# Layer 0 of a four-layer graph network: shared tiles of early states, and an earlier store of states

## The chip, the cores and the metric

The kernel runs on one core of one Trainium2 chip. The metric is the device time of one execution in microseconds. The kernel before was run three times: median 3316.09 us, lowest 3314.98, highest 3317.21. One more execution was recorded by the hardware profiler. It took 3310.86 us, of which 3309.1 us lie between the first and the last instruction (the span).

## What is computed

A batch of 64 graphs with 256 nodes each and 256 features per node goes through four layers. After each layer the result is added to its input and normalised over the features. Layers 1 to 3 are a graph convolution, a masked attention with one head and a masked attention with eight heads; the change doesn't touch them. Layer 0 is a recurrence over the nodes, in the order of their numbers:

```python
def step(h, i):
    x = jnp.take(h_e, i, axis=1)
    row = jnp.take(norm_adjT, i, axis=1)
    x_par = jnp.einsum('bj,bjd->bd', row, h)
    iou = x @ W_ioux.T + b_ioux + x_par @ W_iouh.T + b_iouh
    r, z = jnp.split(iou, 2, axis=1)
    r, z = (jax.nn.sigmoid(r), jax.nn.sigmoid(z))
    hc = jnp.tanh(x @ W_coux.T + b_coux + x_par * r @ W_couh.T + b_couh)
    h_new = z * x_par + (1.0 - z) * hc
    h = jax.lax.dynamic_update_slice(h, h_new[:, None, :], (0, i, 0))
```

`h` starts as the input and is overwritten node by node, so node i sees the new states of nodes before it and the inputs of all others, each weighted by an entry of the adjacency matrix.

## The kernel before

**The recurrence.** The loop `for now in range(N)` takes the 256 nodes one after the other; n is the node, and one pass is called a step here. Each step is a chain of small operations (transposition of `xp`, L612; gate products, L605; sigmoids; the candidate's product; the next `xp`), and no step can begin before the one ahead of it has ended. Eight steps make a round (U = 8), and a node's place in its round is p = n % 8. Thirty-two nodes make a block (T = 32; k is the block, i the place in it).

**Where the weighted sums come from.** The sum over the other nodes is split by distance:

- Inputs of nodes not yet reached: products of adjacency and inputs, stored in DRAM as `Us`. The second half of them is still being worked off during the first steps (`x_side`).
- The nearest states: VectorE and GpSimd operations (`push`, L630, and `push_far`, L663 and L667).
- States some way back: the *late side*. The last 64 states stay on chip in a ring, `Hw`; a state enters it through `into_ring` (L656, four small transfers in every step at the places 4 to 7), and `late` (L521) multiplies the ring with a table `An` in the steps at the places 0 to 3. At place 0 this product already needs the state of two nodes before. The result goes to DRAM and back with the axes turned (`Lb`, L501; `late_sb`, L507), and GpSimd adds it at places 6 and 7 (L876).
- States still further back: the *early side*. Whole states are copied from the ring to DRAM (`Hd`, by `flush`, L638). For a target block k, a range lo to hi of earlier nodes and a group t of eight graphs, `early_load` brings a tile `Hs` of states back from `Hd`, 8 KB for each row, and for every second group a tile `A` of the adjacency matrix in runs of 128 B. `early_fill` (L418) multiplies them at the places 4 to 7, eight times for each tile, and the results go to DRAM as `Es` (L430). `early_in_part` (L447) reads them back at place 0, two rounds ahead of their nodes.

**The order of the work.** The order on each engine is the order of the Python program (`manual_schedule`). Nearly all transfers of the recurrence are issued by one queue, SyncE's, strictly in that order. Loads that may wait stand in a list, `loads`, sorted by rank (early side 1, tables of the next block 1.5, inputs of `x_side` 2), and two of them are issued in each step at the places 0 to 3 (`next_load`). `landed` holds back an early product until its loads were issued three steps earlier. Products waiting to be copied out of PSUM stand in `copies`; stores that follow them run one step later (`at_step`).

**The early side's list.** Eight pieces (first node n, target k, lo, hi), each with eight groups t, make 64 tiles `Hs` and 32 tiles `A`. Two target blocks use the same states in two cases: k = 4 and k = 6 both need nodes 0 to 79, and k = 5 and k = 7 both need nodes 0 to 111. Each of them loads its own copy. Four tiles `Hs` fit at a time (pool `wide`, four buffers).

**The table of the next block.** `late_load` (L479 cuts it) and `load_S` queue their loads at i = 0. GpSimd cuts `An` at i = 12, 15, 20 and 23; if a part of the table hasn't been issued by then, the cut issues it first:

```python
            def cut(lo):
                while not all(begun):
                    next_load(now)
```

**The end.** `n == N - 40` asserts that the lists are empty, and the weights of the other layers are then queued. After the last node the layers run over the 64 graphs, reading states from `Hd`.

Of the kernel before, what the change touches and what calls it, by code (L numbers as in the profile page):

```python
# [9 lines left out]
F32 = mybir.dt.float32  # L10
# [9 lines left out]
P = 128  # L20
# [50 lines left out]
def _recurrence(tc, ident, Hd, x, adj, W_ioux, b_ioux, W_iouh, b_iouh, W_coux, b_coux, W_couh, b_couh, wide, then):  # L71
# [19 lines left out]
    nc = tc.nc  # L91
    B, N, D = x.shape
    T = 32
# [3 lines left out]
    W = 2 * T  # L97
    GB = 8
    XB = 4
    NG = B // 4  # L100
    HB = B // 2
    FAR = (2, 4, 4, 4, 4, 4, 3, 4)

    with ExitStack() as ctx:
# [12 lines left out]
        Hw = const.tile([P, HB, D], F32, name="Hw")  # L117

        def ring(lo, hi):

            while lo < hi:
                end = min(hi, (lo // W + 1) * W)
                yield lo, end, lo % W
                lo = end
# [138 lines left out]
        def load_later(out, in_, rank):  # L263

            begun = []

            def f(n):
                with nc.allow_non_contiguous_dma(reason="bias vector across partitions"):
                    nc.sync.dma_start(out, in_)
                begun.append(n)  # L270

            loads.append((rank, f))
            loads.sort(key=lambda e: e[0])
            return begun
# [47 lines left out]
        def x_side():  # L322
# [39 lines left out]

        early = [
            (n, k, lo, hi, t)
            for n, k, lo, hi in (
                (25, 2, 0, 16), (57, 3, 0, 48), (89, 4, 0, 80), (121, 5, 0, 112), (89, 6, 0, 80),
                (153, 6, 80, 144), (121, 7, 0, 112), (185, 7, 112, 176),
            )  # L370
            for t in range(B // GB)
        ]
        early_in = []
        early_pb = []
        early_ub = []
        Es = {}

        def early_load(e, got=[]):

            _, k, lo, hi, t = early.pop(e)  # L380
            rows = hi - lo
            if t == 0:
                Es[k, lo] = dram.tile([2, NG, 4, T, P], F32, name=f"Es_{k}_{lo}", bufs=1)
            Hs = wide.tile([P, GB, D], F32, tag="wide", name=f"Hs_{k}_{lo}_{t}")
            last = [load_later(
                Hs[0:rows], Hd[lo:hi, t * GB:(t + 1) * GB, :], 1
            )]
            if t % 2 == 0:
                A = stream.tile([P, 2 * GB, T], F32, tag="A", name=f"A_{k}_{lo}_{t}")
                last.append(load_later(  # L390
                    A[0:rows],
                    adj[t * GB:(t + 2) * GB, lo:hi, k * T:(k + 1) * T].rearrange("b j i -> j b i"), 1
                ))
                got[:] = [A]
            early_in.append((last, k, lo, hi, t, Hs, *got))

        def early_ahead(n):
            ready = [e for e, piece in enumerate(early) if piece[0] <= n]
            if len(early_in) < 4 and ready:

                half = [e for e in ready if early[e][4] % 2 and early[e - 1:e] != [
                    early[e][0:4] + (early[e][4] - 1,)
                ]]
                early_load((half + ready)[0])

        def early_fill(n):

# [156 lines left out]
        def load_x(a):  # L564

            xq = stream.tile([P, U // 2, D], F32, tag="xq", name=f"xq_{a}")
            for h in range(2):
                at = a * U + h * U // 2
                nc.sync.dma_start(xq[h * B:(h + 1) * B], x[:, at:at + U // 2, :])
            return xq  # L570
# [46 lines left out]
        def new(tag, n, bufs=2):  # L617
            return work.tile([P, P], F32, tag=tag, name=f"{tag}_{n}", bufs=bufs)
# [14 lines left out]

        def flush(lo, hi):

            for lo, hi, at in ring(max(lo, 0), hi):
                for g in range(2):
                    nc.sync.dma_start(  # L638
                        Hd[lo:hi, g * HB:(g + 1) * HB, :],
                        Hw[g * W + at:g * W + at + hi - lo],  # L640
                    )

        def state(n):

            h = keep[:, n % 2, :]
            nc.vector.tensor_add(h, zcc, keep[:, 2, :])
            hs = new("hs", n, 7)
            nc.vector.tensor_add(hs, zcc, keep[:, 2, :])
            ring_in.append((n, hs))
            return hs  # L650
# [29 lines left out]
        with tc.tile_pool(name="r_first_ps", bufs=4, space=bass.MemoryType.PSUM) as xps:  # L680
            for g in range(0, B, GB):
                A, Xs = first_in.pop(0)
# [74 lines left out]
        for now in range(N):  # L757
            n = now
            k, i = divmod(n, T)
            p = n % U  # L760
            last = n + 1 == N
# [5 lines left out]
            if n:  # L767

                assert all(j == n - 2 for _, j in pushes)
                hs = state(n - 1)  # L770
                end = min((n - 1) // U * U + 2 * U, N)
# [30 lines left out]
            if not last:  # L802
                kk, ii = divmod(n + 1, T)
                ready = new("ready", n, 1)
# [9 lines left out]
            if p in (3, 4):  # L814
                half = slice((p - 3) * U // 2, (p - 2) * U // 2)
# [57 lines left out]
            if p in (6, 7) and n + 8 - p in sides:  # L873
                half = slice(0, U // 2) if p == 6 else slice(U // 2, U)
# [9 lines left out]
                sums_in(n // U + 3)  # L884
            if p == 2 and n // U + 2 < N // U:
                xq[n // U + 2] = load_x(n // U + 2)
            if i == 24:
                flush(n - 8 - T, n - 8)
            if n == N - U + 3:
                assert all(j >= N - U for j, _ in ring_in)  # L890
                flush(N - T // 2, N - U)
            if n == N - 5 * U:
                assert not early and not early_in and not loads
                then(lambda to, of: load_later(to, of, 3))
            early_ahead(n)
            if k + 1 < NB:
                if i == 0:
# [563 lines left out]
def kernel(ctx: ExitStack, tc: tile.TileContext, ins, out):  # L1461
# [14 lines left out]
    def load_layers(load):  # L1476
        weights.extend(
            _load_layers(nc, wide, load, ins["L1_gnn_W"], ins["L1_gnn_b"], l2, l3)
        )

    _recurrence(
        tc, ident, Hd, x, adj,
        *(ins["L0_gnn_" + n] for n in (
# [44 lines left out]
```

## Time and profile before

| | us |
|---|---|
| median of three runs | 3316.09 |
| profiled execution, whole | 3310.86 |
| its span | 3309.1 |
| TensorE busy | 3078.2 (93%) |
| VectorE busy | 2627.0 (79%) |
| GpSimd busy | 1922.6 (58%) |
| ScalarE busy | 1833.1 (55%) |
| first node's transposition (L612) starts | 137.3 |
| last node's transposition starts | 1467.9 |

The recurrence thus takes some 1330 us of the span; the layers after it take most of the rest. The transfers in it that concern the change are:

| transfer | issues | KB each |
|---|---|---|
| `Hs` from `Hd` | 64 | 128, 384, 512, 640 or 896 |
| `A` | 32 | 32 to 224 |
| `Hd` from `Hw` (`flush`) | 24 | 256, 512 or 1024 |
| `Hw` from `hs` (`into_ring`) | 496 | 32 |
| `Es` from `eu` | 64 | 256 |

An engine that is busy 93% of the time isn't the limit for that reason: in the recurrence each step waits for its own results. What ends late is found by looking at single steps, at what TensorE waits for in a long one, and at what SyncE's queue was doing then.

### The profile page before, as it was taken

To read this page: it belongs to the slowest core of one execution; us is meant where nothing else is said; L and a number is where in the kernel's file an instruction comes from. 1 tells how busy PE (TensorE), PEld (TensorE's weight loads), DVE (VectorE), ACT (ScalarE), POOL (GpSimd) and SP (SyncE) were. 2 spreads that over 40 slices of the span, in tenths; PEclk is the share of its full clock that TensorE was granted. 3 is DMA by queue.
4 is the path that set the end of the run, shared out by engine and by line. 5 is a ranking of instruction groups with operands and counts; after the bars stand their busy time and mean duration, and the time that the engine had idled before them with its cause. 6 is when DMAs were issued, how large, how long until landed. Compare 5 with 4: busy or idle time off the path is not lost.

```text
span 3309.1 us, 80053 instructions
## 1 busy us (share of the span) xinstructions
PE 3078.2 (93%) x28332; PEld 2275.6 (69%) x28332; DVE 2627.0 (79%) x7511; ACT 1833.1 (55%) x4690; POOL 1922.6 (58%) x2230
## 2 busy tenths in 40 slices
PE   5799998989889898977999999999999999999997
PEld 4566665555555555645888888888888888888885
DVE  3478877777677877855888888888888888888885
ACT  0155554544444454534666666666666666666664
POOL 2377777766566888843555555555555555555543
PEclk8899999999899999998999999999999999999999
DMA  9856686788777575334333333333333333333310
GB/s 292 253 159 156 169 196 159 175 194 207 188 195 176 149 188 149 98 79 96 74 77 78 78 81 78 78 78 77 77 77 79 77 78 77 78 77 77 78 43 20
DMA packets 807146, 398.31 MB, mean 120 GB/s; under 512 B 525148, under 2 KB 773096, under 8 KB 801512
## 3 DMA queue, kind: packets, MB, share of 16 engines
q1 hardware_dynamic: 789048, 376.25, 46.4%
q10 hardware_dynamic: 17696, 16.91, 1.5%
q8 instruction: 227, 3.72, 0.5%
q14 instruction: 175, 1.43, 0.1%
HBM read 274.34 MB, written 99.61 MB: 113 GB/s over the span
## 4 chain that ended last, share of the span: by engine, by line
PE 80%; DMA 7%; DVE 7%; issue 2%; SPq 2%; ACT 1%; POOL 1%; ACTq 0%; DVEq 0%; POOLq 0%
PE mm L1005 14%; PE rc L605 7%; PE rc L597 5%; PE s L1231 4%; PE late L521 4%; PE mm_3v L1005 4%; PE mm_2f L1005 4%; PE mm_2v L1005 3%; PE mm_3f L1005 3%; PE mm_g L1005 3%; PE mm_2s L1005 3%; PE mm_2w L1005 3%; PE mm_t L1005 3%; PE o L1266 3%; DVE ACC L630 3%; PE z_ps L605 2%
## 5 line engine op out<-in xcount | busy, mean ns | idle before, releaser
L1243 POOL TENSOR_TENSOR p3s<-p 128x256 f32<-128x256 f32 x512 | 358.5, 732 | 270.8 <-ACT p L1241 270.4
L630 DVE SCALAR_TENSOR_TENSOR ACC<-keep,S,ACC 128x128 f32<-128x128 f32 x1712 | 479.2, 343 | 16.7 <-POOL ACC L876 10.9
L1005 PE MATMUL mm<-xT,weights 128*128 128x256 f32 x2048 | 483.8, 384 | 2.7 <-ACT xT L1121 2.7
L1005 PEld LDWEIGHTS mm<-xT,weights 128*128 128x128 f32 x2048 | 386.1, 191 | 80.2 <-ACT xT L1121 28.8
L667 POOL TENSOR_TENSOR ACC<-ACC,far 128x384 f32<-128x384 f32 (+1 forms) x313 | 371.8, 1188 | 24.6
L1240 DVE TENSOR_TENSOR p<-s,neg 128x512 f32<-128x512 f32 x512 | 317.7, 683 | 85.2 <-PE s L1231 85.2
L961 ACT ACTIVATE y<-y,shift,rstd 128x256 f32<-128x256 f32 x512 | 279.5, 596 | 156.8 <-DVE shift L959 156.7
L1241 ACT ACTIVATE p<-p 128x512 f32<-128x512 f32 x512 | 307.0, 629 | 3.6 <-DVE p L1240 3.0
L663 POOL TENSOR_TENSOR far<-hs,S 128x384 f32<-128x384 f32 (+1 forms) x313 | 304.2, 972 | 4.7
L597 PE MATMUL rc<-WxT,xqT 128*64 128x256 f32 x2048 | 275.6, 390 | 0.7 <-issue 0.7
L805 POOL TENSOR_TENSOR ready<-ACC,dinv 128x128 f32<-128x128 f32 x255 | 101.8, 399 | 299.1 <-DVE ACC L630 298.4
L953 POOL TENSOR_TENSOR rstd<-rstd,mhalf 128x2 f32<-128x2 f32 x256 | 173.5, 695 | 133.5 <-DVE rstd L952 131.8
L1280 DVE RECIPROCAL rT<-o 128x256 f32<-128x256 f32 x128 | 223.7, 1748 | 0.0
L949 DVE BATCH_NORM_STATS2 st<-y 128x6 f32<-128x256 f32 x512 | 209.6, 409 | 12.5 <-POOL y L1142 9.7
L1142 POOL TENSOR_TENSOR y<-y,g 128x512 f32<-128x512 f32 x64 | 81.2, 1268 | 216.4 <-ACT g L1139 196.8
L824 ACT ACTIVATE rs<-rc 128x128 f32<-128x128 f32 x256 | 70.9, 277 | 244.4 <-PE rc L605 244.4
L605 PE MATMUL rc<-WhT,rT 128*64 128x128 f32 x2048 | 172.3, 289 | 35.3 <-DVE rT L828 31.6
L521 PE MATMUL late<-Hw,An 64*32 64x256 f32 x3840 | 165.5, 399 | 37.8 <-DMA Hw<-hs 14.3
L605 PEld LDWEIGHTS rc<-WhT,rT 128*64 128x64 f32 x2048 | 108.7, 138 | 133.0 <-DVE rT L828 109.7
L1153 ACT ACTIVATE qk<-mm,weights 128x256 f32<-128x256 f32 x256 | 107.2, 470 | 160.9 <-PE mm L1005 159.0
L605 PE MATMUL rc<-WhT,xpT 128*64 128x128 f32 x2048 | 169.7, 287 | 19.0 <-ACT xpT L614 19.0
L597 PEld LDWEIGHTS rc<-WxT,xqT 128*64 128x64 f32 x2048 | 140.6, 140 | 54.9 <-ACT rc L861 10.7
(168 smaller groups left out, 7205.4 us busy)
## 6 DMA issues: line engine op xcount, KB each, us to landing
xX<-in_x_dram ACTq DMA_DIRECT2D x16, 1024.0 KB
Us<-xu SPq DMA_DIRECT2D x64, 256.0 KB
xq<-in_x_dram SPq DMA_DIRECT2D x64, 256.0 KB
ACC<-Us SPq DMA_DIRECT2D x32, 512.0 KB
Es<-eu SPq DMA_DIRECT2D x64, 256.0 KB
early_sb<-Es SPq DMA_DIRECT2D x32, 512.0 KB
xin<-in_x_dram SPq DMA_DIRECT2D x64, 256.0 KB
ad<-in_adj_dram SPq DMA_DIRECT2D x64, 256.0 KB
```

Of the source, the lines that this page charges most:

```text
L521: nc.tensor.matmul(pb[g][q * T:(q + 1) * T, e, :], An[rows, b].rearrange("p u s -> p (u s)"), Hw[rows, b, :], start=True, stop=True,)
L597: nc.tensor.matmul(G[o * B:(o + 1) * B], xqT[a, i // 2][:, i % 2, kc, h * B:(h + 1) * B], WxT[:, kc, o, gates], start=False, stop=False, s ...
L605: nc.tensor.matmul(G[o * B:(o + 1) * B], hT[:, kc * B:(kc + 1) * B], WhT[:, kc, o, g], start=False, stop=(kc == 1), skip_group_check=True,)
L630: nc.vector.scalar_tensor_tensor(acc[:, 0, :], keep[:, j % 2, :], s, acc[:, 0, :], ALU.mult, ALU.add)
L663: nc.gpsimd.tensor_mul(tmp[:, 0:count, :], hs.unsqueeze(1).to_broadcast(shape), s.unsqueeze(2).to_broadcast(shape),)
L667: nc.gpsimd.tensor_add(acc, acc, tmp[:, 0:count, :])
L961: nc.scalar.activation(y[:, c, :], y[:, c, :], AF.Identity, bias=shift[:, c:c + 1], scale=rstd[:, c:c + 1],)
L1005: nc.tensor.matmul(pm[:, c, :], lhsT[:, k, c * P:(c + 1) * P], rhs[:, k, :], start=(k == 0), stop=(k == 1),)
L1240: nc.vector.tensor_add(p, s_ps[i], self.neg3)
L1241: nc.scalar.activation(p, p, AF.Exp, scale=ISQ)
L1243: nc.gpsimd.tensor_add(both, p[:, 0, :], p[:, 1, :])
L1280: nc.vector.reciprocal(rT, o_ps[:, 1, :])
```

## The change

Three things are changed.

1. The early side's list is put in a new order. Pieces that need the same states stand together, and their groups alternate in pairs ("46464466": a pair of groups for k = 4, the same pair for k = 6, and so on). A tile `Hs` that is already on chip for the same range and group is used again; a list `states_in` keeps the tiles, and a new one is loaded only if the oldest of the last four is no longer needed. At most two pairs are on hand before another pair is begun.
2. States are stored to DRAM at i = 16 of every block and no longer at i = 24. The store then covers the 32 nodes before this one. The newest of them isn't in the ring yet, and goes to `Hd` directly from its tile (`state_out`, two transfers).
3. The transfers of `flush` are cut at every 16 nodes and no longer only at the ring's end. The early side's pieces may begin seven nodes sooner (18, 50, 82, ... for 25, 57, 89, ...).

```diff
-        early = [
-            (n, k, lo, hi, t)
-            for n, k, lo, hi in (
-                (25, 2, 0, 16), (57, 3, 0, 48), (89, 4, 0, 80), (121, 5, 0, 112), (89, 6, 0, 80),
-                (153, 6, 80, 144), (121, 7, 0, 112), (185, 7, 112, 176),
-            )
-            for t in range(B // GB)
-        ]
+        early = []
+        for n, lo, hi, order in (
+            (18, 0, 16, "2222"), (50, 0, 48, "3333"), (82, 0, 80, "46464466"),
+            (114, 0, 112, "57575577"), (146, 80, 144, "6666"), (178, 112, 176, "7777"),
+        ):
+            for e, k in enumerate(order):
+                u = order[:e].count(k)
+                early += [(n, int(k), lo, hi, 2 * u), (n, int(k), lo, hi, 2 * u + 1)]
...
+        early_A = []
+        states_in = []
...
-            Hs = wide.tile([P, GB, D], F32, tag="wide", name=f"Hs_{k}_{lo}_{t}")
-            last = [load_later(
-                Hs[0:rows], Hd[lo:hi, t * GB:(t + 1) * GB, :], 1
-            )]
+            if not any(e[0] == (hi, t) for e in states_in):
+                Hs = wide.tile([P, GB, D], F32, tag="wide", name=f"Hs_{hi}_{t}")
+                states_in.append(((hi, t), Hs, load_later(
+                    Hs[0:rows], Hd[lo:hi, t * GB:(t + 1) * GB, :], 1
+                )))
+            _, Hs, begun = next(e for e in states_in if e[0] == (hi, t))
...
         def early_ahead(n):
-            ready = [e for e, piece in enumerate(early) if piece[0] <= n]
-            if len(early_in) < 4 and ready:
-
-                half = [e for e in ready if early[e][4] % 2 and early[e - 1:e] != [
-                    early[e][0:4] + (early[e][4] - 1,)
-                ]]
-                early_load((half + ready)[0])
+            if not early or early[0][0] > n:
+                return
+            _, _, _, hi, t = early[0]
+            units = {(e[1], e[2], e[4] // 2) for e in early_in}
+            if t % 2 == 0 and len(units) > 1:
+                return
+            if len(states_in) >= 4 and not any(e[0] == (hi, t) for e in states_in):
+                old = states_in[-4][0]
+                if any(old == (e[3], e[4]) for e in early_in + early):
+                    return
+            early_load(*early.pop(0))
...
         def flush(lo, hi):
 
-            for lo, hi, at in ring(max(lo, 0), hi):
+            for lo in range(max(lo, 0), hi, T // 2):
+                end = min(hi, lo + T // 2)
                 for g in range(2):
+                    at = g * W + lo % W
                     nc.sync.dma_start(
-                        Hd[lo:hi, g * HB:(g + 1) * HB, :],
-                        Hw[g * W + at:g * W + at + hi - lo],
-                    )
+                        Hd[lo:end, g * HB:(g + 1) * HB, :], Hw[at:at + end - lo]
+                    )
+
+        def state_out(n, hs):
+            for o in range(2):
+                nc.sync.dma_start(Hd[n][:, o * P:(o + 1) * P], hs[o * B:(o + 1) * B])
...
-            if i == 24:
-                flush(n - 8 - T, n - 8)
+            if i == T // 2:
+                state_out(n - 1, hs)
+                flush(n - T, n - 1)
```

More of the change, by code (lines that the diff above doesn't have):

```diff
@@ L375, in _recurrence, with early_load @@
         early_ub = []
+        early_A = []
+        states_in = []
         Es = {}
-        def early_load(e, got=[]):
-            _, k, lo, hi, t = early.pop(e)
+        def early_load(n, k, lo, hi, t):
             rows = hi - lo
-            if t == 0:
+            if (k, lo) not in Es:
                 Es[k, lo] = dram.tile([2, NG, 4, T, P], F32, name=f"Es_{k}_{lo}", bufs=1)
-            Hs = wide.tile([P, GB, D], F32, tag="wide", name=f"Hs_{k}_{lo}_{t}")
-            last = [load_later(
-                Hs[0:rows], Hd[lo:hi, t * GB:(t + 1) * GB, :], 1
-            )]
+            if not any(e[0] == (hi, t) for e in states_in):
[4 more added lines that the diff above has]
+            _, Hs, begun = next(e for e in states_in if e[0] == (hi, t))
             if t % 2 == 0:
                 A = stream.tile([P, 2 * GB, T], F32, tag="A", name=f"A_{k}_{lo}_{t}")
-                last.append(load_later(
+                early_A[:] = A, load_later(
                     A[0:rows],
                     adj[t * GB:(t + 2) * GB, lo:hi, k * T:(k + 1) * T].rearrange("b j i -> j b i"), 1
-                ))
-                got[:] = [A]
-            early_in.append((last, k, lo, hi, t, Hs, *got))
+                )
+            early_in.append(((begun, early_A[1]), k, lo, hi, t, Hs, early_A[0]))
         def early_ahead(n):
-            ready = [e for e, piece in enumerate(early) if piece[0] <= n]
-            if len(early_in) < 4 and ready:
-                half = [e for e in ready if early[e][4] % 2 and early[e - 1:e] != [
-                    early[e][0:4] + (early[e][4] - 1,)
-                ]]
-                early_load((half + ready)[0])
+            if not early or early[0][0] > n:
[9 more added lines that the diff above has]
+            early_load(*early.pop(0))
         def early_fill(n):
```

## The prediction, made before the changed kernel was run

> **What bounds the kernel now.** I read the page first. TensorE is busy 93% of the span, but that share covers two stages. The change lies in the first, the recurrence, which ends near slice 18 of 40. There the transfer share and the granted clock stand out:
>
> ```profile
> span 3309.1 us, 80053 instructions
> ...
> PEclk8899999999899999998999999999999999999999
> DMA  9856686788777575334333333333333333333310
> ```
>
> The transfers fill seven to eight tenths of slices 8 to 12, against three tenths in the later layers. Next I took the start of each node's transposition (L612) from the timeline, and so the length of every step. Quiet steps repeat within a few ns: 4.38 us with no filler work, 4.64 with two early products' halves, 4.81 at places 1 and 2, 5.44 at place 0. Against the shortest step of the same place and content, the steps from node 8 on lose 95.5 us in all. A handful of long steps hold nearly all of it. Rounds of equal TensorE work show this in the view of windows (columns: stretch, length, busy time of PE, PEld, DVE, ACT and POOL, granted clock, transfer share, GB/s):
>
> ```profile
> 546.74:584.95 38.21, 34.53 (x475) 22.69 (x473) 33.30 (x121) 19.51 (x67) 29.70 (x35) 1.00 0.47 130
> 718.24:757.54 39.30, 38.81 (x538) 23.97 (x537) 33.45 (x121) 21.46 (x70) 29.87 (x35) 1.00 0.82 197
> 846.75:903.30 56.55, 43.55 (x538) 25.97 (x536) 31.87 (x114) 21.49 (x70) 31.05 (x34) 0.85 0.81 191
> 903.30:943.12 39.82, 38.96 (x538) 24.07 (x536) 33.83 (x121) 21.39 (x70) 29.94 (x35) 1.00 0.85 215
> 943.12:995.32 52.20, 42.77 (x539) 25.79 (x537) 32.75 (x118) 21.47 (x70) 31.57 (x35) 0.91 0.77 186
> ```
>
> 538 matmuls take 39.3 us or 56.55. So neither TensorE nor the recurrence's arithmetic is late in the bad rounds. The view of waits over the recurrence names what is:
>
> ```profile
> POOL ACC L876 <- DMA late_sb<-Lb: 16.6, 7, 6.4
> PE late L521 <- DMA Hw<-hs: 14.3, 7, 4.8
> PE late L521 <- DMA A<-in_adj_dram: 10.6, 3, 5.8
> POOL An L479 <- DMA raw<-in_adj_dram: 10.3, 1, 10.3
> ```
>
> One such step (node 72, 13.2 us for 5.44) on TensorE, and SyncE's queue beside it:
>
> ```profile
> 500.50 0.33 PE L826 MATMUL rT_ps<-ident,rs 128*128 128x128 f32 x1
> 506.62 1.23 PE L521 MATMUL late<-Hw,An 64*32 64x256 f32 x16 [5.79 <-DMA A<-in_adj_dram]
> 507.78 1.12 PE L605 MATMUL rc<-WhT,rT 128*64 128x128 f32 x8
> ```
>
> ```profile
> 496.38 0.92 SPq L430 DMA_DIRECT2D Es<-eu  x1
> 497.39 2.88 SPq L656 DMA_DIRECT2D Hw<-hs  x4
> 500.38 0.60 SPq L269 DMA_DIRECT2D Hs<-Hd  x1
> 501.08 0.37 SPq L269 DMA_DIRECT2D A<-in_adj_dram  x1
> 501.56 1.71 SPq L430 DMA_DIRECT2D Es<-eu  x2
> ```
>
> The late product doesn't read `A`; it waits for the ring's last write, issued at 499.58, whose semaphore fills at 506.38. In quiet steps at place 0 that write is issued 2.6 to 3.9 us before the step begins; here SyncE's queue was 0.9 us past its beginning, and the write then shared the engines with `Hs`, `A` and `Es`. After the gap TensorE's products take 0.81 us for 0.41, so 5.8 us of waiting cost 7.8. I read one root under these stalls: SyncE's queue running late in a flood of transfers. They show in three ways: at place 0 (ring, 45.7 us over the recurrence), at place 7 (`late_sb`, 10.5) and at the cut of `An` (places 5 and 6, 15.3). Another 14.7 are in eight other steps, the rest in small change.
>
> **What the Trainium skill says.** DMA: Bandwidth & Descriptors, in the section Why a DMA increments its semaphore by 16 and not by 1, states that a transfer runs on the largest number of engines up to 16 that divides its outermost dimensions, each of which reports separately. The trace agrees for the ring's write, whose outer dimension is 2: three events each, one at issue and two later. A flush of 15 rows would thus use 15 engines, one of 31 rows only one; the cut at 16 nodes gives pieces of 16 and 15. The same page (Issuing engines are not separate DMA queues) says all transfers share the same 16 engines, which the windows at a share of 0.8 bear out. TensorE: Matmul & The Clock Gate, Part 1, puts the array at half clock after an idle window of some 3.4 us; the trace's 0.41 to 0.81 us after gaps agrees.
>
> **The change, part by part.** *Loads removed.* Stepping through the rules of the list gives 48 `Hs` loads for 64: eight of 80 rows and eight of 112 rows are gone, 1536 rows of 8 KB, 12.6 MB. A packet of 8192 B took 539 ns in the mean at 600 to 1000 us, so 1536 x 0.539 / 16 = 52 us of all 16 engines. SyncE loses 16 issues of 0.6 us, most of them longer when the queue is full (up to 11 us for one).
>
> *Store moved and cut.* Bytes are the same (packets of 32 KB, 2.3 us each, about 9 us of all engines for a block). Issues go from 24 to 32, and 16 for `state_out` are new: 24 x 0.5 = 12 us of SyncE's time over eight blocks, at place 0, where the queue has three steps until the ring's next write. New waits: the flush now reads a row written one place earlier, but that write has landed, since the late product of the same step needed it too. And at nodes 112 and 144 the last `Es` of the block is stored in the very step that reads it back, so SyncE waits for it to land. Behind it stand `state_out`, the flush and the sums' load for three rounds later. The nearest row is SyncE's L507 waiting for `Lb`, 18.5 us over 19 waits, longest 1.8; between 0.5 and 5 us each, I take 3. Only two `A` are loaded in those rounds, so I cost it at nothing; without this cover it is the slower case below.
>
> *Work moved.* Early halves stay 128 in 64 steps. By the step lengths above, their places and those of the input products sum to 598.2 us for 600.4: -2, within what filler lengths are known, so I take zero. `x_side` ends at node 87 for 79; its rows are first needed at node 105.
>
> *Load by round.* With each transfer at its packet time in the trace (128 B 16 ns, 512 B 28, 4 KB 237, 8 KB 540), a round's transfers in us of 16 engines, before and after: from node 80 on 16/32, 29/21, 32/29, 35/32, 31/29, 40/26, 39/33, 41/39, 36/30, 39/25, and from 160 to 216 together 208/200. A round lasts about 40, so the rounds from 120 to 152 were full, and one stays near it. How load turns into stalls I can only read from before, and I did so twice. By classes: rounds above 36 lost 9.4 us in the mean (five), those of 30 to 36 lost 2.7, of 24 to 30 some 3, below 24 some 0.5. That gives 91 us for the rounds from 48 on before and 60 after: -30. Round by round: place 0 at 104 from 7.3 to 3.5 (3.4 us less ahead of it), 128 and 152 from 11.7 to 1, 136 from 7.3 to 5, 160 from 5.6 to 0.5, 72 nearly kept, the later ones a little worse as they no longer follow a long pause: 45.7 to 22. `late_sb` from 10.5 to 1. The cut: the last part of `raw` is issued at place 3 of nodes 107 and 139 and no longer by the cut itself a step later, so 15.3 becomes 6. The others 14.7 to 12. Together 86 to 41: -45. I take the middle, -38. What is late next is then the recurrence itself at its quiet lengths, and the stalls at 72, 136 and 144.
>
> The profiled execution took 3310.9 us (span 3309.1); with -38 it is 3273. The median of the runs lies 5.2 above it, which gives 3278.
>
> **The rivals.** *Expected (70%):* stalls in the shared rounds fall, -15 to -62, so 3254 to 3301.
>
> *The gain is given back (15%):* the queue regulates itself. A stall is also a pause in which transfers catch up: after 56.55 us came a round of 39.82 at the same load. If the same bytes still come in bursts, stalls move to other rounds (72 lost 7.8 us in a round of only 28). Speaks against it: five of the six worst rounds are those that lose bytes. From -15 to +7; about 3312.
>
> *Slower (12%):* the earlier store. Seven times, 31 rows of 64 KB start at place 0 of the round in which the tables `S` and `raw` follow, or the last inputs do (rounds 48 and 80 go from 25 to 35 and from 16 to 32 us of load), with SyncE also waiting for `Es` at 112 and 144. If each flush makes the ring or `late_sb` of its round miss, at 8 us (the mean of long place 0 steps), six of them cost 48. Against the gain of 38 this is +10: 3326, up to +40. It decides once more than five flush rounds miss. Against it: rounds with a flush before (24, 56, 88) were followed by 0 to 2.5 us.
>
> *The change doesn't do what it says (3%):* sharing fails because tiles are evicted. Stepping through the rules shows every second load of the shared ranges gone, so this leaves only errors of mine; about 3316.
>
> **How the numbers follow.** Differences under 0.2%, 6.6 us, can't be told from none. Faster: 70 and half of the second case (7), 77%. Same: 6 of the second and the last 3, 9%. Slower: 12 and the remaining 2, 14%. The range 3250 to 3318 takes in the expected case and the second one, and leaves out most of the slower one.
>
> **What would show it.** Right: 48 loads of `Hs`; the transfer share of 600 to 1000 us under 0.75 for 0.81; steps at nodes 128, 152 and 160 near 5.5 us, no long steps at 127, 141 and 159; `late` waiting about 12 us for `Hw` and `A`, for the 24.9 of the two lines above; the layers after the recurrence unchanged. Wrong: long steps at nodes 48 to 56, 80 to 88, 112 to 120 and 144 to 152, with SyncE waiting at L447 or L638, or long place 0 steps in as many rounds as before.

## The result, and the profile after

The kernel after took 3328.05 us (median of six runs, 3326.34 to 3333.09), the kernel before, beside it, 3314.55 (six runs, 3309.23 to 3317.21). The ratio is 1.0040, with a 95% interval from 1.0028 to 1.0053: slower by 13.5 us, where a gain of 38 us was forecast. The time lies above the range.

The page of the kernel after:

```profile
span 3326.6 us, 80047 instructions
...
PEclk8899989999999999997999999999999999999998
DMA  9864556686866675334233333333333333333310
```

The transfers fill less of slices 8 to 12 than before, as meant (48 loads of `Hs`; from 600 to 1000 us a share of 0.72 for 0.81). The span is 17.5 us longer all the same. The last node's transposition starts at 1484.3 us, 16.4 us later than before, and the first one at the same 137.3: the loss lies in the recurrence.

Round by round, measured from transposition to transposition, the gain and the loss stand side by side (us):

| round from node | 24 | 48 | 56 | 72 | 80 | 104 | 112 | 136 | 144 | 152 |
|---|---|---|---|---|---|---|---|---|---|---|
| before | 39.5 | 40.3 | 41.0 | 48.0 | 38.2 | 52.5 | 39.3 | 56.6 | 39.8 | 52.2 |
| after | 51.0 | 51.1 | 55.1 | 40.1 | 47.8 | 39.5 | 50.6 | 43.9 | 53.6 | 39.1 |

The rounds at 72, 104, 136 and 152, those that the prediction wanted to mend, are mended and more: 209.3 us became 162.6. But six quiet rounds have become slow. The view of windows of the kernel after shows the rounds 104, 112, 136 and 144 (columns as in the prediction):

```profile
709.72:749.25 39.53, 38.88 (x538) 23.98 (x536) 31.88 (x114) 21.41 (x70) 30.25 (x34) 1.00 0.86 196
749.25:799.84 50.59, 42.06 (x538) 25.71 (x537) 33.53 (x121) 21.52 (x70) 30.24 (x35) 0.90 0.65 159
878.72:922.61 43.89, 38.95 (x539) 24.00 (x537) 31.78 (x114) 21.40 (x70) 30.23 (x34) 1.00 0.88 215
922.61:976.20 53.59, 42.90 (x538) 25.94 (x536) 33.53 (x121) 21.51 (x70) 30.23 (x35) 0.87 0.62 152
```

The slow rounds are the ones with the *lower* transfer share. Share times length is nearly the same in the first two, 34 and 33 us of all engines: about as much transfer work, spread over a longer round. How full the transfer engines are over a round doesn't say whether the round is late. What is late is said by the view of waits over the recurrence (150 to 1470 us; total, times, longest). Line numbers are those of the kernel shown: L521 of the kernel before is L527 here, and L531 where an experiment adds four lines.

```profile
DVE deg L304 <- DMA rows<-in_adj_dram: 34.1, 6, 9.3
...
ACT xu L256 <- DMA Us<-xu: 13.9, 5, 7.6
ACT eu L256 <- DMA Es<-eu: 12.4, 4, 3.8
...
PE late L527 <- DMA Hw<-hs: 9.2, 5, 4.0
```

The last line is one of the waits behind the long steps of the kernel before (14.3 us there), and `late_sb` is gone from the list. The first three are new, or have grown. The same view of the kernel before has no wait for `Es`, and of the other two:

```profile
ACT xu L256 <- DMA Us<-xu: 4.0, 2, 2.4
...
DVE deg L304 <- DMA rows<-in_adj_dram: 0.3, 1, 0.3
```

**First new wait: rows behind the store.** Node 116 (place 4, 11.8 us for 4.64). SyncE's queue ahead of it:

```profile
752.86 1.79 SPq L436 DMA_DIRECT2D Es<-eu  x2
757.06 0.34 SPq L453 DMA_DIRECT2D early_sb<-Es  x1
757.49 1.13 SPq L652 DMA_DIRECT2D Hd<-hs  x2
758.67 7.48 SPq L646 DMA_DIRECT2D Hd<-Hw  x4
766.19 2.03 SPq L316 DMA_DIRECT2D ACC<-Us  x1
768.33 3.52 SPq L301 DMA_DIRECT2D rows<-in_adj_dram  x2
```

VectorE and TensorE at the same time:

```profile
773.12 0.35 DVE L877 SCALAR_TENSOR_TENSOR xp<-zcc,Sd,keep 128x128 f32<-128x128 f32 x1
778.69 0.69 DVE L304 TENSOR_REDUCE deg<-rows 128x2 f32<-128x512 f32 x1 [5.22 <-DMA rows<-in_adj_dram]
...
781.37 0.28 DVE L839 TENSOR_TENSOR rT<-rT_ps,xpT 128x128 f32<-128x128 f32 x1
```

```profile
775.71 0.64 PE L424 MATMUL early<-Hs,A 80*32 80x256 f32 x8
781.71 1.12 PE L611 MATMUL rc<-WhT,rT 128*64 128x128 f32 x8 [5.36 <-DVE rT L839]
```

`flush` holds SyncE's queue for 7.5 us here, and for 7.0 to 10.1 us in each block with a full flush. Behind it stands the load of adjacency rows (`rows`, L301), of which VectorE makes the degrees for the block after (L304) as background work. Its last rows are issued up to 771.9 us and summed at 778.7. VectorE works in the program's order, so the small product `rT` of the running step stands behind that sum, and TensorE waits for `rT`. The load has nothing to do with the early side, and the step doesn't need the degrees. The same happens at place 4 in all six rounds in which a full flush has rows behind it (nodes 52, 84, 116, 148, 180 and 212): together 46.6 us above the quiet length, of which the rows' wait is 34.1.

**Second new wait: the output buffers.** Node 56 (14.6 us for 5.44). ScalarE, then SyncE's queue:

```profile
443.94 0.59 ACT L256 COPY xu<-xp 128x512 f32<-128x512 f32 x1
452.13 0.59 ACT L256 COPY xu<-xp 128x512 f32<-128x512 f32 x1 [7.60 <-DMA Us<-xu]
452.61 0.27 ACT L620 COPY xpT<-xpT_ps 128x128 f32<-128x128 f32 x1
```

```profile
444.56 0.93 SPq L220 DMA_DIRECT2D Us<-xu  x2
445.53 0.52 SPq L453 DMA_DIRECT2D early_sb<-Es  x1
446.09 3.27 SPq L238 DMA_DIRECT2D dinv<-deg  x4
```

`x_side` and the early side share two output buffers (`stream.tile(tag="ub")`). A buffer is held from the copy of the first tile of a pair to the store of the pair. Only the first of the two tiles is in at node 54; it is multiplied there, and the second not before node 60. By the program, the place at which the pieces now start makes the difference. Loads are issued at the places 0 to 3 alone, two in each step. Pieces that began at node 57 (place 1) had two more such steps in their round; those that begin at node 50 (place 2) have one, enough for the first tile and `A`. The second tile's load comes in the next round:

```profile
418.60 0.58 SPq L269 DMA_DIRECT2D Hs<-Hd  x1
420.52 0.35 SPq L269 DMA_DIRECT2D A<-in_adj_dram  x1
...
442.84 0.94 SPq L269 DMA_DIRECT2D Hs<-Hd  x2
```

For that round one of the two buffers is taken, and the copies of `x_side` follow each other on the other one: the copy at 452.13 waits for a store that was issued only after the copy at 443.94. ScalarE's copy of `xpT`, which the step needs, stands behind it. In the long steps at nodes 24, 30, 39, 56, 62 and 71 ScalarE waits in such a copy for a store of `Us` or `Es`; they lose 31 us together.

**A smaller one: nodes 112 and 144.** The late product waits there for the ring's last write (2.9 and 4.0 us), and the steps take 9.7 and 10.8 us for 5.44. In every kernel below with shared tiles these two steps take 7.6 to 12.4 us, in those with own tiles (before, experiments 1, 5 and 6) 5.4 to 6.1. So a loss of 10 us in the kernel after goes with the sharing; why the write is late there stays open.

### The profile page after: what moved, and what is told of

Its sections match the earlier page's. It is cut to its first block, busy times and chain, and to the rows that moved or that the text cites. A ratio compares the mean times of both kernels' runs of the same rounds, so it can differ in the third digit from the quotient of the medians.

```text
span 3326.6 us, 80047 instructions
## 1 busy us (share of the span) xinstructions
PE 3083.6 (93%) x28332; PEld 2279.5 (69%) x28332; DVE 2625.7 (79%) x7511; ACT 1834.3 (55%) x4690; POOL 1924.5 (58%) x2230
## 4 chain that ended last, share of the span: by engine, by line
PE 79%; DVE 8%; DMA 7%; issue 2%; ACT 1%; SPq 1%; POOL 1%; DVEq 0%; ACTq 0%; POOLq 0%
PE mm L1017 14%; PE rc L611 7%; PE rc L603 4%; PE s L1243 4%; PE mm_3v L1017 4%; PE mm_2f L1017 4%; PE mm_2v L1017 3%; PE mm_3f L1017 3%; PE mm_t L1017 3%; PE late L527 3%; PE mm_g L1017 3%; PE mm_2w L1017 3%; PE mm_2s L1017 3%; PE o L1278 3%; DVE ACC L636 3%; PE z_ps L611 3%
## 5 line engine op out<-in xcount | busy, mean ns | idle before, releaser
L611 PEld LDWEIGHTS rc<-WhT,xpT 128*64 128x64 f32 x2048 | 107.0, 136 | 120.7 <-ACT xpT L620 110.1
L839 DVE TENSOR_TENSOR rT<-rT_ps,xpT 128x128 f32<-128x128 f32 x256 | 74.2, 290 | 141.6 <-PE rT_ps L837 139.1
```

The costliest lines, as they stand in the source:

```text
L611: nc.tensor.matmul(G[o * B:(o + 1) * B], hT[:, kc * B:(kc + 1) * B], WhT[:, kc, o, g], start=False, stop=(kc == 1), skip_group_check=True,)
```

## The experiments

Theory: two things that the prediction put at nothing cost about 50 us together, and the sharing itself brings what was forecast. (a) The flush at i = 16 stands ahead of the rows in SyncE's queue. (b) A pair of tiles that straddles a round takes an output buffer away. Rivals: the new order of the list itself is bad; sharing brings little; or the rows are only the first to be late of a whole queue. Kernels of one batch ran on one chip beside the kernel before (medians 3315.66, 3315.77 and 3316.92 us). All microseconds "against before" below are the measured ratio less 1, times 3315; taken from the medians alone they shift by up to 4 us.

**1. The store alone.** The kernel before with the earlier store, cut at 16 nodes; the old list and old loads.

```diff
-            if i == 24:
-                flush(n - 8 - T, n - 8)
+            if i == T // 2:
+                state_out(n - 1, hs)
+                flush(n - T, n - 1)
```

> The kernel before with the earlier, cut store alone (store at i = 16, state_out, pieces of 16 nodes); the early side's list and its 64 loads of states are those of before. My theory now: the flush at i = 16 stands in SyncE's queue ahead of the degree rows that are loaded at i = 17 and summed by VectorE at place 4 of the same round, so VectorE waits 3 to 10 us there in seven rounds. Then this kernel has these long steps at nodes 20 or 52, 84, 116, 148, 180, 212, VectorE waits some 34 us for the rows, ScalarE waits no more than before (some 4 us) for the copies' stores, and the time is 3340 to 3360. Rival (the new list is what makes the changed kernel slower, the store is harmless): 3305 to 3318, no wait for the rows.

Measured: 3336.22 us, ratio 1.0063 (1.0040 to 1.0086), a little under the expected range. Its view of waits:

```profile
DVE deg L304 <- DMA rows<-in_adj_dram: 44.2, 6, 16.2
...
ACT xu L256 <- DMA Us<-xu: 3.3, 2, 1.7
```

The rows' wait comes with the store and without the new list; the output buffers' wait doesn't.

**2. The rows ahead of the flush.** The kernel after with `flush` one step later, behind the background block that issues the rows.

```diff
                 state_out(n - 1, hs)
-                flush(n - T, n - 1)
...
+            if i == T // 2 + 1:
+                flush(n - 1 - T, n - 2)
```

> The changed kernel with the flush issued one step later, at i = 17, behind the degree rows' load; state_out stays at i = 16. My theory: the long steps at place 4 (47 us in the profile of the changed kernel) go almost whole, VectorE's wait for rows falls from 34 us to under 5, and the time is 3280 to 3292. Rival (the flush's traffic as such costs the time, wherever it is issued within the round): the stalls move to the ring, late_sb or the copies, and the time stays within 3318 to 3335.

Measured: 3311.16 us, ratio 0.9987 (0.9976 to 0.9999): between the two expectations, and less than half of the gain expected. The rows' wait is gone from the list, but:

```profile
ACT xu L256 <- DMA Us<-xu: 17.0, 5, 8.6
...
ACT eu L256 <- DMA Es<-eu: 13.2, 4, 3.7
...
POOL ACC L887 <- DMA late_sb<-Lb: 12.3, 3, 8.2
```

The output buffers' waits have grown from 26.3 to 30.2 us, and `late_sb` has come back. The position of the flush is worth some 18 us and not the 47 that the six steps lose. A reading that fits, and that experiment 7 bears on: a long step is also time in which the queue catches up.

**3. Whole pairs only.** The kernel after, with a pair begun only when both of its tiles are in.

```diff
                 if not early_in or not landed(early_in[0][0], n):
                     return False
+                if early_in[0][4] % 2 == 0 and (
+                    len(early_in) < 2 or not landed(early_in[1][0], n)
+                ):
+                    return False
```

> The changed kernel, but the first half of a pair of early tiles is multiplied only once both tiles of the pair are in, so that no pair holds one of the two output buffers (ub) over a round. My theory: ScalarE's copies no longer wait for stores of Es and Us (26 us of waits in the changed kernel, some 31 us of long steps at nodes 24, 30, 56, 62 and 71), and the time is 3295 to 3308; the long steps at place 4 stay. Rival (the stores land late because of the flush and would be waited for anyhow): ScalarE's waits stay above 15 us, the time within 3318 to 3332.

Measured: 3295.07 us, ratio 0.9929 (0.9905 to 0.9953), at the low end of what was expected and faster than both kernels. Waits (the profiled execution is the slowest of the six, 12 us above the median):

```profile
DVE deg L304 <- DMA rows<-in_adj_dram: 23.7, 5, 8.1
...
ACT xu L256 <- DMA Us<-xu: 4.8, 3, 2.2
```

No wait for `Es` is left and `xu` waits about as long as before the change; the rows still wait in the flush rounds. The second wait thus goes with the straddling pair.

**4. Both.** Experiments 2 and 3 together.

> Both edits together: flush behind the rows' load, and pairs multiplied only when whole. If the two waits are independent, the time is 3250 to 3268, faster than both kernels by more than 1.4%. Rival (queue regulates itself, what is taken away in one place comes back in another): above 3285.

Measured: 3276.91 us, ratio 0.9878 (0.9840 to 0.9917). Between the two expectations: 40 us under before, but not the 48 or more that I thought. What remains are steps at place 0 (nodes 112, 144, 152, 168, 184 and 200 at 9.5 to 12.2 us) and two at place 7.

**5. The store a step later, in the old list.** Experiment 1 with `flush` at i = 17, as in experiment 2.

> The kernel before (its list, 64 loads of states) with state_out at i = 16 and the cut flush at i = 17 behind the degree rows. Against the kernel with the store alone at i = 16 it differs in nothing but the one step. If the rows behind the flush are what makes the store cost time, it is back at the kernel before: 3305 to 3322, VectorE's wait for rows under 5 us. Rival (an earlier store costs time by its traffic in any position): 3328 to 3345.

Measured: 3317.54 us, ratio 0.9998 (0.9984 to 1.0011). VectorE's wait for the rows is 1.0 us, for 44.2 in experiment 1. Storing seven steps sooner, `state_out` and the cut at 16 nodes cost nothing together, within some 5 us; one step sooner still, ahead of the rows, costs 22 us.

**6. Own tiles.** Experiment 4 with every target block loading its own tile: same list, same steps of the early products, 64 loads.

```diff
-            if not any(e[0] == (hi, t) for e in states_in):
+            if not any(e[0] == (hi, t, k) for e in states_in):
...
-            _, Hs, begun = next(e for e in states_in if e[0] == (hi, t))
+            _, Hs, begun = next(e for e in states_in if e[0] == (hi, t, k))
```

> The kernel with both edits (flush behind the rows, whole pairs only), but every target block loads its own tile of states: 64 loads for 48, in the same order, and each product at the same step. It measures what the sharing alone is worth. My prediction's reading was that the 16 loads cost some 38 us of stalls: then 3305 to 3325, with long steps at place 0 and at the cut of An back between nodes 104 and 160. Rival (the new order and the later cut of raw bring the gain, not the sharing): within 8 us of the kernel with both edits, 3270 to 3285.

Measured: 3316.91 us, ratio 1.0003 (0.9993 to 1.0013). The windows from 600 to 1000 us, first of this kernel, then of experiment 4:

```profile
600.00:1000.00 400.00, 350.05 (x4579) 213.93 (x4579) 275.75 (x983) 183.93 (x602) 256.90 (x281) 0.94 0.76 189
```

```profile
600.00:1000.00 400.00, 381.21 (x5142) 233.58 (x5140) 309.80 (x1101) 206.41 (x675) 288.33 (x316) 0.98 0.72 178
```

With shared tiles 5142 matmuls are done in the stretch that sees 4579 without. Sharing alone is worth 41 us (0.9878 against 1.0003), give or take 13 by the intervals. The new order with whole pairs brings nothing by itself.

**7. The sums later.** The kernel after, with the last two sums of the rows two steps later (and the arithmetic behind them one). If the rows alone were late, giving them time would do what experiment 2 does.

```diff
-                if i in (0, 2, 3, 8, 10, 11, 12, 15, 16, 17, 19, 20, 22, 24):
+                if i in (0, 2, 3, 8, 10, 11, 12, 15, 16, 17, 21, 22, 23, 24):
```

> The changed kernel with the flush where it is, but VectorE's sums of the last degree rows two steps later (i = 21 and 22 for 19 and 20; the reciprocal at 23). If the stall at place 4 is the consumer coming due two steps after its load was queued behind the flush, the wait for rows falls from 34 us to under 8 and the time to 3280 to 3310. Rival (the whole queue is late, not only the rows): long steps at places 4 to 7 stay, 3320 to 3335.

Measured: 3332.69 us, ratio 1.0051 (1.0034 to 1.0067): a miss. Waits:

```profile
POOL ACC L887 <- DMA late_sb<-Lb: 27.0, 7, 8.1
...
ACT xu L256 <- DMA Us<-xu: 17.9, 5, 9.3
PE late L527 <- DMA Hw<-hs: 17.6, 7, 4.0
...
DVE deg L304 <- DMA rows<-in_adj_dram: 0.3, 1, 0.3
```

The rows' wait is gone and the time isn't. `late_sb`, absent from the kernel after, waits 27 us instead, and `Hw` 17.6 for 9.2: those stand further back in the queue behind the flush. The rival was right: more than the rows is late behind the flush, and the rows were only the first to be needed.

**8. The store in two halves.** Experiment 4 with the older 16 nodes stored at i = 9.

```diff
+            if i == 9:
+                flush(n - 9 - T // 2, n - 9)
             if i == T // 2 + 1:
-                flush(n - 1 - T, n - 2)
+                flush(n - 1 - T // 2, n - 2)
```

> The kernel with both edits, and the older half of each flush (16 nodes, long in the ring) issued at i = 9 and no longer at i = 17 with the younger half. If what is left of the stalls in the flush rounds (nodes 55, 87, 112, 152, 184: 23 us in its profile) comes from 2 MB in one burst, the time is 3260 to 3272. Rival (the burst at i = 9 meets the ring's writes of its own round and only moves the stalls): 3273 to 3285.

Measured: 3266.14 us, ratio 0.9848 (0.9825 to 0.9871), as expected and the lowest of all: 50 us under before. Against experiment 4 that is 10 us, but the two intervals overlap, so the split's own share isn't shown.

**9. Half a store ahead of the rows.** Experiment 3 with the older half at i = 9, and the younger one at i = 16 ahead of the rows, as in the kernel after. It asks whether order or size does the harm.

> Whole pairs, the older half of the flush at i = 9 as in the split store, but the younger half at i = 16, ahead of the degree rows: 1 MB stands before them and no longer 2. If it is the size of the burst that matters, the time is that of the split store, 3262 to 3273. If it is the rows standing behind any flush, VectorE waits for them again at place 4 (10 us or more in all) and the time is 3276 to 3290.

Measured: 3275.41 us, ratio 0.9863 (0.9842 to 0.9884), between the two expectations; the rows wait 5.4 us in all. Its interval overlaps that of experiment 8, so a half store ahead of the rows costs some 15 us at most, and may cost nothing. It costs less than the whole one at the same place, with which experiment 3 has 0.9929.

**10. Whole pairs, early blocks only.** The rule of experiment 3 for blocks 2 and 3 alone, where `x_side` still uses the output buffers beside the early side. A rival to (b) was that the rule helps because the first products start later everywhere.

```diff
-                if early_in[0][4] % 2 == 0 and (
+                if early_in[0][1] < 4 and early_in[0][4] % 2 == 0 and (
```

> The changed kernel with the rule of whole pairs for the target blocks 2 and 3 alone, the only ones worked on while the input products also fill output buffers. If the two output buffers are the cause, it gains what the rule gains everywhere: 3288 to 3303, with ScalarE's waits for the stores of Es and Us under 8 us. Rival (the rule helps by beginning the shared pieces later): 3315 to 3330.

Measured: 3299.60 us, ratio 0.9941 (0.9924 to 0.9958). ScalarE's waits for the stores of `Us` and `Es` are 6.7 us, for 26.3 in the kernel after. Nearly the whole gain (the intervals overlap) comes from the blocks where two sides share two buffers.

## Why the prediction was wrong

The runs give the sum below, in us against before. Each line is the difference of two kernels that differ by that edit, uncertain by 5 to 15 us, from their intervals. The sum closes by construction; what tests it is the same edit between other kernels, in the last column.

| step | us | same edit elsewhere |
|---|---|---|
| store sooner, cut, flush at i = 17 (experiment 5) | -0.7 | |
| new list, whole pairs, own tiles (5 to 6) | +1.7 | |
| shared tiles (6 to 4) | -41.4 | |
| flush at i = 16, ahead of the rows (4 to 3) | +16.9 | +18 (2 to after), +22 (5 to 1) |
| pairs may straddle a round (3 to after) | +36.8 | +36 (4 to 2) |
| sum: the kernel after | +13.3 | |

**"Loads removed".** Right: 48 loads, -41 us for -38. **"Load by round"** had the right total and, in large part, the wrong place. By the place in the round, the steps that are over 0.4 us too long lose, in one profile each (us; counted by place alone, so the ring's 45.7 us are part of 50.2; the last column takes in the small excesses too):

| | 0 | 1 to 3 | 4 | 5 | 6 | 7 | all steps |
|---|---|---|---|---|---|---|---|
| before | 50.2 | 10.9 | 0.5 | 11.3 | 5.6 | 10.5 | 95.5 |
| after | 29.9 | 6.6 | 47.1 | 5.5 | 11.8 | 7.0 | 114.6 |
| own tiles (6) | 47.8 | 4.5 | 11.0 | 10.7 | 3.9 | 18.4 | 101.9 |
| shared tiles (4) | 43.9 | 1.2 | 0 | 0.7 | 0 | 10.9 | 64.2 |
| store in halves (8) | 22.1 | 13.4 | 0 | 6.9 | 2.2 | 0 | 51.4 |

"45.7 to 22" was to be the main gain at place 0. Between experiments 6 and 4, place 0 falls by 4 us; of the 38 us in the last column 32 are won at the places 4 to 7. That place 0 stands at 29.9 in the kernel after shows little, as its new stalls may give the queue pauses; among the three kernels at the foot of the table, which have few or none of these, it falls to about 22 only where the store is also split. So the agreement of -38 with -41 is of the total and not of its parts, and in that partly luck.

**"Store moved and cut ... I cost it at nothing".** This step failed, worth 17 to 22 us. It had the issues (24 more of 0.5 us) but not how long the flush holds the queue: 7.5 us for its four issues at node 112. The kernel before could have told. Its flush at nodes 87 and 88 has four issues, that at node 183 two with the same 2 MB:

```profile
583.38 9.80 SPq L638 DMA_DIRECT2D Hd<-Hw  x4
...
1118.44 0.88 SPq L638 DMA_DIRECT2D Hd<-Hw  x2
1119.37 8.46 SPq L238 DMA_DIRECT2D dinv<-deg  x4
```

Either way the queue is held for some 9 us, in the second case mostly by the four small transfers that follow. After the first of these flushes no step of the round is long (nodes 88 to 95), so a hold alone needn't do harm; it depends on what stands behind it. The prediction named what stands behind as "`state_out`, the flush and the sums' load for three rounds later" and looked for the next ring write three steps on. The rows (L301), due to be issued at the end of the next step and to be summed two steps after that, weren't on the list. Where the kernel before issued the last of them in the steps 81, 113 and 145, the kernel after did so in 83, 115 and 147. The wait for `Es` that it did price, at 3 us, is there and about right: at node 112 SyncE's issues pause for 2.4 us ahead of `early_sb`, from 754.65 to 757.06.

**"Work moved ... I take zero".** This step failed too, and it was the dearer one, 36 to 37 us. It counted TensorE's filler, for which zero is right (experiment 6). It never asked what else an early product holds: an output buffer from the first tile of a pair to the second. Starting at place 2 and no longer at place 1 brings the first tile in at a place 6 at which the second isn't.

**The slower rival** said that "each flush makes the ring or `late_sb` of its round miss, at 8 us", six times, and so 3326. Six flush rounds did miss, at 7.8 us each, but it was VectorE's sum that missed; `late_sb` did so only in other kernels (12.3 us in experiment 2, 27.0 in experiment 7). And of those 47 us only 17 to 22 are the flush's net cost. That its 3326 lies near 3328.05 is therefore in large part chance: the larger part of the loss is the buffers', which no case had. The wrong signs in the list of what to watch, long steps in the rounds at 48, 80, 112 and 144, did show.

**"An", "late_sb" and the ring.** At the nodes that were to get better, they did: steps at 128, 152 and 160 take 5.44 us, 127 and 159 4.64; node 141 kept 3.3 us. `late` waits 9.2 us for `Hw` and 4.2 for `A`, where about 12 were forecast. But 6.7 us of its waits are now put down to `raw`, which the list of before doesn't have for `late`, so that all three make 20.1 us for 24.9: the ring's lateness moved in part (to nodes 112 and 144 for one). The kernel after is slower although every long step that the prediction wanted to shorten became shorter.

**A reading that doesn't hold as stated.** "0.81 us for 0.41" after the gap at node 72 isn't what the lines shown there give: eight products of L605 take 1.12 us for 0.66. The half clock itself is there, a granted clock of 0.50 from 505 to 510 us, so what the prediction built on it stands.

**What stays open.** Some long steps show no cause: node 18, behind the first flush, takes 9.6 us in the kernel after, and the profile shows only "issue" ahead of TensorE; experiment 8 has four such (163, 171, 179, 211). Whether the burst's size or its place counts isn't settled between experiments 8 and 9, nor was a flush of two larger writes tried at i = 16. A third output buffer, which would test the second wait from the other side, wasn't tried, and neither were pieces that start at place 1 again.

## What to carry to other kernels

When a transfer is moved in a queue, write down everything issued behind it for as long as it takes to land, background work too, and look up for each who waits and what stands behind that waiter; the engine that is hurt here, VectorE, had no part in the change. When work is begun sooner, ask what it holds while it is half done: a pair begun with one tile there kept one of two buffers and cost twice what the moved store did. And don't read lateness off the share of busy transfer engines alone: rounds of 39.5 us at 0.86 and of 50.6 us at 0.65 had the same matmuls and about as much transfer work.

## What the runs showed that I hadn't expected

Four large writes held SyncE's queue for 7.5 us at their issue, and not evenly: at node 112 the first two took 0.6 and 0.4 us, the last two 2.6 and 3.8, where those of `Es` just ahead (L436) took 0.9 each. With two writes at a time (experiment 8) a half flush took 0.8 to 1.9 us. The delay of the rows is one of the queue more than of the engines: these rows were issued by 771.9 us, 13 us after the flush began; from issue to landing they took 8 to 9 us, not far from the 4.5 to 8.7 of the rows elsewhere in the same kernel, with the engines at a share of 0.98.

The Trainium skill (DMA: Bandwidth & Descriptors, Issuing engines are not separate DMA queues) calls the time of initiating a transfer "usually small relative to the DMA itself" and says that all transfers interleave on the same 16 engines. The second is what the trace shows: by the semaphores the first of the rows landed from 773.0 us on, while the flush's last write landed until 773.2. The first holds for the first two writes (0.6 and 0.4 us at the issue, of 6.8 and 9.5 from issue to landing) and less for the last two (2.6 and 3.8 of 10.9). But issues of one queue add up: of the 20 us from the flush's first issue to the rows' sum, 13.2 had passed when the queue had issued the rows.

Long steps aren't additive. The six steps behind the rows lose 47 us and their cause is worth 17 to 22; moving the rows' sums away won back nothing, and waits that had been absent appeared in its place (experiment 7). The reading that a stall lets the queue catch up fits this; it wasn't tested by itself.
